# Layer 1's second attention: the last edge type's scores from its weights, and the first softmaxes issued during the last projection

## The chip, the cores and the metric

The kernel runs on one core of a Trainium2 chip. The metric is the device time of one execution in microseconds (us); lower is better. Times given for a kernel are medians over its executions. Beside them stands one profiled execution, in which every instruction has a start and a duration.

The engines are named as in the profile: PE is the matrix engine (TensorE; PEld its weight loads), DVE is VectorE, ACT is ScalarE, POOL is GpSimd, SP is the engine that issues most of the loads. Each engine works through its own list of instructions in order and waits for the others by semaphores.

## The reference

Four graph layers work on 512 nodes with 768 features, over 8704 edges, each followed by a residual sum and a layer norm: a graph attention (layer 0), a relational attention with three edge types (layer 1), a relational convolution (layer 2) and a graph convolution (layer 3). The change is in layer 1, in the second of its two attentions (one head, 768 channels):

```python
def rgat_conv(x, W, q, k, b, src, dst, etype, heads, out_ch, n_nodes):
    xr = jnp.einsum('nd,rdf->rnf', x, W)      # one projection for each edge type r
    oi = xr[etype, dst]
    oj = xr[etype, src]
    alpha = jax.nn.leaky_relu(oi @ q + oj @ k, NEG_SLOPE)
    m = jax.ops.segment_max(alpha, dst, num_segments=n_nodes)
    e = jnp.exp(alpha - m[dst])
    z = jax.ops.segment_sum(e, dst, num_segments=n_nodes)
    a = e / (z[dst] + EPS)
    msg = (a[:, :, None] * oj.reshape(-1, heads, out_ch)).reshape(-1, heads * out_ch)
    return jax.ops.segment_sum(msg, dst, num_segments=n_nodes) + b

h = jax.nn.elu(rgat_conv(x, W1, q1, k1, b1, src, dst, edge_type, 4, 192, n))
out = rgat_conv(h, W2, q2, k2, b2, src, dst, edge_type, 1, 768, n)
```

For each node and each type there are two scores: the query score `xr @ q` of the node as a destination, and the key score `xr @ k` of the node as a source. `xr[r] @ q` is `h @ (W[r] @ q)` as well.

## The kernel before

**Dense form.** The edges have been counted into 512 x 512 matrices, one for each type, whose logarithms (`log3_store`, in device memory) are added to the scores before the exponential. So one softmax step (`soft`) works on a tile of 128 destination nodes by 3 x 512 sources and types: three activations that add a query score as a bias to a row of key scores (L1370), leaky ReLU (L1373), the log and the maximum (L1375), the exponential (L1379). `turn` transposes the 128 x 1536 tile in twelve 128 x 128 steps on PE (L1395) and copies it out of PSUM (L1399). The sum over sources is twelve matmuls against the projected nodes `xr` for each half of the channels (L1522 in the second attention, L1449 in the first).

**Projections.** `product` computes 512 nodes by 384 columns of one weight matrix in four node blocks. A block is twelve matmuls (L799 and L802: rounded parts and remainders, 6 of each), a scale of the PSUM bank on ACT (L805), and six matmuls of a third form (L810, `rest`). The `rest` of one block is issued behind the first twelve matmuls of the next. Behind each block `product` runs a job, if one is given in `between`, and then `split_piece()`, which cuts the next piece of a third of a half weight matrix into its three forms: one activation on ACT (L756) and two steps on DVE (L757, L758), 768 columns each. The raw pieces come over SP's queue into three buffers, the forms live in two sets. A weight matrix is two such units, j = 0 and 1; a PSUM tile is one of eight banks.

**The second attention.** Six products, for types r = 0, 1, 2 and halves j = 0, 1. Each block is copied out of PSUM into `xr[r]`, whose rows are two halves of 384 with columns of ones beside them, by `evacuate`, which alternates between ACT (L85) and DVE (L87). Behind the second half of a type, `dots` computes both scores of a block on DVE: for each score and each half a multiply with an accumulated sum over 128 x 384 (`dot`, L858), and an add of the halves (L1487). After all six products, `on_all` spreads the key scores of each type over all partitions by transposes of broadcast columns (L866), a copy makes them a row (`kk2`), and `run` goes through the softmax steps:

```python
soft_done, turned = {0: soft_of(0)}, {}
for s in range(-1, steps):
    if 0 < s + 2 < steps:
        soft_done[s + 2] = soft_of(s + 2)
    elif s == -1 and steps > 1:
        soft_done[1] = soft_of(1)
    if s + 1 < steps:
        turned[s + 1] = turn(soft_done.pop(s + 1), f"{soft_of.__name__}{s + 1}")
    if s >= 0:
        sum_of(s, turned.pop(s))
```

The log of a step (786 KB) is loaded by SP into a single buffer. `qk2`, the vectors q and k on all partitions, lies in the tile `kk` of the first attention, reused under the same tag; the scratch row of the dots lies under the tag `elu` of the same pool, in a single buffer.

**What sets the order.** The code is issued in program order with few exceptions; a framework places the instructions on their engines, moves some past others by its own estimates, and sets the semaphores. An engine executes the list that comes out of this strictly in order.

Of the kernel before, what the change touches and what calls it, by code (L numbers as in the profile page):

```python
# [34 lines left out]
def gnn_stack_kernel(ctx: ExitStack, tc: tile.TileContext, a: dict, out: bass.AP):  # L35
# [673 lines left out]
    def split_layers():  # L709
# [111 lines left out]
        def columns_of(j):  # L821
            return slice(j * HD, (j + 1) * HD)
# [40 lines left out]
        def on_all(dst, cols, name):  # L863

            for b in range(NB):
                nc.tensor.transpose(  # L866
                    dst[:, b * P : (b + 1) * P], cols[b].to_broadcast([P, P]), ident
                )


        with (
            tc.tile_pool(name="g", bufs=1) as g,
# [148 lines left out]
            class Head:  # L1021
# [8 lines left out]
                def project(self, jobs=(), halves=(0, 1), late=None):  # L1030

                    if late is None and 0 in halves:
                        self.h = [row_tile(f"{self.name}_h{b}") for b in range(NB)]
                    for j in halves:

                        def keep(b, po, j=j):
                            def fill():
                                nc.scalar.copy(self.h[b][:, columns_of(j)], po[:, :HD])

                            if late is not None:  # L1040
                                late.append(fill)
# [12 lines left out]
                    close_group()  # L1054
# [226 lines left out]
        with (  # L1281
# [57 lines left out]
                    f, *args = waiting.pop(0)  # L1339
                    f(*args)  # L1340

            def project(left, r, j, name, also=None):
                def keep(b, po):
                    evacuate(xr[r][:, b, row_slice(j * HD, (j + 1) * HD)], po[:, :HD])
                    if also and j:
                        also(r, b)

                product(left, keep, f"{name}_p{r}_{j}", [next_job] * NB)

            for r in range(R3):  # L1350
                for j in range(2):
# [50 lines left out]
            def source(k, cs):  # L1402
                return xr[k // NB][:, k % NB, cs]

            def run(steps, soft_of, sum_of):


                soft_done, turned = {0: soft_of(0)}, {}
                for s in range(-1, steps):
                    if 0 < s + 2 < steps:  # L1410
                        soft_done[s + 2] = soft_of(s + 2)
                    elif s == -1 and steps > 1:
                        soft_done[1] = soft_of(1)
                    if s + 1 < steps:
                        turned[s + 1] = turn(soft_done.pop(s + 1), f"{soft_of.__name__}{s + 1}")
                    if s >= 0:
                        sum_of(s, turned.pop(s))

            def brow_of(v, name):
                return row_on_all(rp, v, name, "brow")  # L1420
# [15 lines left out]
            def sum1(s, wT):  # L1436
# [29 lines left out]
            run(NB * H1, soft1, sum1)  # L1466
            finish1(NB - 1)

            qk2 = rp.tile([P, H1, R3, N], F32, tag="kk", name="r2_qk").rearrange(
                "p h r n -> p (h r n)"  # L1470
            )
            qk2 = [qk2[:, i * D : (i + 1) * D] for i in range(2)]
            for t, v in zip(qk2, (a["L1_gnn_q2"], a["L1_gnn_k2"])):
                nc.gpsimd.dma_start(t, bass.AP(tensor=v.tensor, offset=v.offset, ap=[[0, P], [1, D]]))
            cols2 = rp.tile([P, 2, R3, NB], F32, tag="cols2", name="r2_cols")
            parts2 = rp.tile([P, 2, 2, R3, NB], F32, tag="parts2", name="r2_parts")

            def dots(r, b):
                for s in range(2):
                    for j in range(2):  # L1480
                        js = row_slice(j * HD, (j + 1) * HD)
                        junk = rp.tile([P, D], F32, tag="elu", name=f"r2_j{r}_{b}_{s}_{j}")
                        dot(
                            parts2[:, j, s, r, b : b + 1], xr[r][:, b, js],
                            qk2[s][:, columns_of(j)], junk[:, :HD],
                        )
                nc.vector.tensor_add(  # L1487
                    cols2[:, :, r, b], parts2[:, 0, :, r, b], parts2[:, 1, :, r, b]
                )

            for r in range(R3):
                for j in range(2):
                    project(S, r, j, "r2", dots)
            close_group()
            kk2 = rp.tile([P, H1, R3, N], F32, tag="kk", name="r2_kk")
            for r in range(R3):
                pk = bank(f"r2_k{r}")
                on_all(pk, [cols2[:, 1, r, b : b + 1] for b in range(NB)], f"r2_k{r}")
                evacuate(kk2[:, 0, r, :], pk)
            brow = brow_of(a["L1_gnn_b2"], "r2_b")  # L1500

            def soft2(b):
                return soft(
                    load_log(b, "r2"), kk2[:, 0], lambda r: cols2[:, 0, r, b : b + 1], f"r2_{b}"
                )

            def finish2(b):
# [297 lines left out]
```

## Time and profile before

| | |
|---|---|
| time before | 1730.66 us, median of 3 (1727.88 to 1731.09) |
| the profiled execution | 1729.9 us, of which its span, first to last instruction, 1727.1 us |
| busy in the span | PE 1614.3, PEld 1443.7, DVE 1187.5, ACT 767.8, POOL 54.2 us |
| projections of the second attention, 937.0 to 1014.2 us | PE busy 77.16 of 77.2, DVE 60.35, ACT 30.27 us |
| from there to the first sum, 1014.2 to 1039.6 us | PE busy 7.32 of 25.4, DVE 17.95, ACT 12.79 us |
| granted TensorE clock, mean | 0.97 |

The page gives for each engine the time in which it executed an instruction; waits are not busy. A list of instructions in order of time gives start, duration, engine, line, operation and operands, and in brackets how long the engine sat idle before it and which instruction released it. The granted clock is the share of full clock that PE was given in a stretch. Line numbers are those of the kernel before; behind line 866 the changed kernel's are some 40 to 60 higher.

### The profile page before, as it was taken

How to read it: one execution, taken by the hardware profiler on the slowest of the kernel's cores; microseconds unless marked ns; L12 is line 12 of the kernel's file. 1: busy time of each engine (PE TensorE's matmuls, PEld its weight loads, DVE VectorE, ACT ScalarE, POOL GpSimd, SP SyncE). 2: the span in 40 equal slices, each digit the busy share in tenths (PEclk: the TensorE clock that was granted, in tenths of full speed). 3: DMA queues.
4: the chain of work that ended last, by engine and by line, in shares of the span. 5: the costliest groups of instructions: out<-in, count | busy, mean ns of one | idle time of the engine just before them, and what ended most of it. 6: DMA issues, size and time to landing. Idle time of an engine off the chain costs nothing.

```text
span 1727.1 us, 22203 instructions
## 1 busy us (share of the span) xinstructions
PE 1614.3 (93%) x8527; PEld 1443.7 (84%) x8527; DVE 1187.5 (69%) x2212; ACT 767.8 (44%) x1321; POOL 54.2 (3%) x71
## 2 busy tenths in 40 slices
PE   5999999999999995999788959999999999999897
PEld 2868879797887964899788956699999999999897
DVE  8977888796868778554784874565666546654764
ACT  5756556554555542243773442233324232423232
POOL 0000000000000002000001000000000002000001
PEclk9999999999999997999799989999999999999999
DMA  3323223131321232222011321232233224332321
GB/s 120 101 71 101 89 89 123 54 103 53 101 64 65 83 91 64 84 74 65 19 38 65 102 82 64 114 119 89 92 104 110 89 80 141 104 95 80 109 63 57
DMA packets 78850, 147.21 MB, mean 85 GB/s; under 512 B 5656, under 2 KB 65936, under 8 KB 76944
## 3 DMA queue, kind: packets, MB, share of 16 engines
q1 hardware_dynamic: 74416, 123.60, 23.2%
q0 software_dynamic: 3600, 20.47, 3.4%
q8 instruction: 69, 1.13, 0.3%
q10 hardware_dynamic: 720, 1.64, 0.3%
q14 instruction: 45, 0.37, 0.1%
HBM read 128.91 MB, written 16.78 MB: 84 GB/s over the span
## 4 chain that ended last, share of the span: by engine, by line
PE 82%; DVE 9%; ACT 4%; DMA 2%; issue 1%; ACTq 0%; DVEq 0%
PE g_o L1061 10%; PE c_p L810 6%; PE c_p L802 6%; PE c_p L799 6%; PE c_a L1565 4%; PE c_a L1569 4%; PE g_s L799 4%; PE g_s L802 4%; PE r_o L1522 4%; PE g_s L810 3%; PE r_p L799 3%; PE r_p L802 3%; PE r_p L810 3%; PE g_p L799 3%; PE g_p L802 3%; PE g_p L810 2%
## 5 line engine op out<-in xcount | busy, mean ns | idle before, releaser
L757 DVE SCALAR_TENSOR_TENSOR w<-w,raw 128x768 fp32r<-128x768 f32 x234 | 222.1, 954 | 116.1 <-ACT w L756 115.0
L756 ACT ACTIVATE w<-raw 128x768 fp32r<-128x768 f32 x234 | 194.8, 839 | 126.2 <-PE c_p L799 34.3
L758 DVE TENSOR_TENSOR w<-w,w 128x768 fp32r<-128x768 f32 x234 | 219.1, 951 | 1.8 <-PE g_p L810 1.0
L802 PE MATMUL c_p<-w,s 128*128 128x384 f32 x576 | 192.5, 334 | 0.0
L799 PE MATMUL c_p<-w,s 128*128 128x384 f32 x576 | 192.5, 334 | 0.0
L1061 PE MATMUL g_o<-wT,g_h 128*128 128x512 f32 x384 | 166.8, 594 | 5.9 <-ACT wT L1017 5.9
L1061 PEld LDWEIGHTS g_o<-wT,g_h 128*128 128x128 f32 x384 | 72.3, 190 | 95.5 <-issue 85.9
L1553 DVE TENSOR_TENSOR c_h_lo<-c_p,c_h_hi 128x384 fp32r<-128x384 f32 x96 | 53.2, 554 | 129.9 <-ACT c_h_hi L1552 129.9
L799 PE MATMUL g_p<-w,s 128*128 128x384 f32 x384 | 134.7, 351 | 0.0
L799 PE MATMUL g_s<-w,y 128*128 128x384 f32 x384 | 131.4, 343 | 0.0
L805 ACT ACTIVATE c_p<-c_p 128x384 f32<-128x384 f32 x96 | 45.6, 475 | 192.9 <-PE c_p L802 192.5
L1565 PE MATMUL c_a<-c_h_hi,c_cT 128*128 128x384 f32 (+1 forms) x384 | 130.5, 340 | 0.0
L802 PE MATMUL g_s<-w,y 128*128 128x384 f32 x384 | 130.0, 339 | 0.0
L802 PE MATMUL g_p<-w,s 128*128 128x384 f32 x384 | 129.7, 338 | 0.1
L1569 PE MATMUL c_a<-c_h_lo,c_cT 128*128 128x384 f32 x384 | 129.8, 338 | 0.0
L810 PE MATMUL c_p<-w,s 128*128 128x384 f32 x576 | 117.9, 339 | 0.0
L799 PEld LDWEIGHTS c_p<-w,s 128*128 128x128 f32 x576 | 108.2, 188 | 0.0
L802 PEld LDWEIGHTS c_p<-w,s 128*128 128x128 f32 x576 | 108.1, 188 | 0.0
L810 PEld LDWEIGHTS c_p<-w,s 128*128 128x128 f32 x576 | 100.0, 188 | 5.3 <-ACT c_p L805 5.3
L799 PE MATMUL r_p<-w,s 128*128 128x384 f32 x288 | 100.0, 347 | 0.0
L802 PE MATMUL r_p<-w,s 128*128 128x384 f32 x288 | 98.5, 342 | 0.0
L810 PE MATMUL g_p<-w,s 128*128 128x384 f32 x384 | 79.4, 340 | 1.5 <-ACT g_p L805 1.4
(259 smaller groups left out, 3278.5 us busy)
## 6 DMA issues: line engine op xcount, KB each, us to landing
raw<-in_L_gnn_W_dram SPq DMA_DIRECT2D x216, 384.0 KB
c_cT<-cT_store POOLq DMA_DIRECT2D x8, 1024.0 KB, 5.7
raw<-in_L_gnn_root_dram SPq DMA_DIRECT2D x18, 384.0 KB
r_log<-log_store SPq DMA_DIRECT2D x8, 768.0 KB
cT_store<-c_cT SPq DMA_DIRECT2D x4, 1024.0 KB
g_s<-in_L_gnn_a_src_dram POOLq DMA_DIRECT2D x8, 384.0 KB, 4.5
g_d<-in_L_gnn_a_dst_dram POOLq DMA_DIRECT2D x8, 384.0 KB, 4.4
log_store<-log SPq DMA_DIRECT2D x12, 256.0 KB
```

The source lines that it names most:

```text
L756: nc.scalar.mul(hm, w, ROUND / SPLIT)
L757: nc.vector.scalar_tensor_tensor(lo, hm, -SPLIT, w, op0=ALU.mult, op1=ALU.add)
L758: nc.vector.tensor_sub(df, hm, lo)
L799: nc.tensor.matmul(po[:, :HD], left[0][:, k, bs], hm[:, k, :], start=(k == 0), stop=False)
L802: nc.tensor.matmul(po[:, :HD], left[1][:, k, bs], lo[:, k, :], start=False, stop=(k == KC - 1))
L805: nc.scalar.mul(po[:, :HD], po[:, :HD], SPLIT + 1.0)
L810: nc.tensor.matmul(po[:, :HD], left[2][:, k, bs], df[:, k, :], start=False, stop=(k == KC - 1), skip_group_check=True,)
L1061: nc.tensor.matmul(po, self.h[k][:, c * P : (c + 1) * P], wT[:, k, :], start=(k == 0), stop=(k == NB - 1),)
L1522: nc.tensor.matmul(po[:, :n], wT[:, k, :], source(k, at), start=(k == 0), stop=(k == NK - 1),)
L1553: nc.vector.tensor_sub(lo, po[:, :HD], hi)
L1565: nc.tensor.matmul(po[:, : HD + ones], cT[:, k, bs], h[0][:, k, : HD + ones], start=(k == 0), stop=False,)
L1569: nc.tensor.matmul(po[:, :HD], cT[:, k, bs], h[1][:, k, :], start=False, stop=(k == NB - 1))
```

## The change

The second attention takes the query and key scores of type 2 no longer from its projected nodes but from its weights. The whole of `W2[2]` (2.36 MB) is loaded a second time, on ACT's queue, into the rest of the tile `kk`, at the end of the first attention. Twelve dots (`last_dots`: six blocks of 128 rows, two scores each) give `W2[2] @ q` and `W2[2] @ k`; `EarlyScores.split` cuts these 128 x 12 numbers into three forms, and `EarlyScores.columns` multiplies them with the forms `S` of all 512 nodes: twelve matmuls with a 2-column stationary tile and 512 moving columns, a scale, six more, a copy, four small transposes. The `dots` of types 0 and 1 work on 768 columns at once, without the adds; those of type 2 are gone. All blocks of the six products are copied out of PSUM by ACT.

The jobs between the blocks issue the rest of it: weight dots during (r, j) = (0, 1) and (1, 0), the score product behind block 2 of (1, 0), the key rows of type 2 behind the first block of (1, 1) and those of types 0 and 1 during (2, 0), softmax steps 0 and 1 during (2, 0), the transposes of step 0 behind block 2 of (2, 1). `run` becomes the class `Steps`, which skips what has been issued. The first attention uses `Steps` too, with nothing issued early.

```diff
+        class EarlyScores:
+            def __init__(self, pool, name):
+                self.name = name
+                self.v = pool.tile([P, 2, KC, 2], F32, tag="early", name=f"{name}_v")
+                self.forms = [
+                    pool.tile([P, KC, 2], F32R, tag=f"early{f}", name=f"{name}_v{f}")
+                    for f in range(3)
+                ]
+
+            def split(self, v):
+                hm, lo, df = self.forms
+                nc.scalar.mul(hm, v, ROUND / SPLIT)
+                nc.vector.scalar_tensor_tensor(lo, hm, -SPLIT, v, op0=ALU.mult, op1=ALU.add)
+                nc.vector.tensor_sub(df, hm, lo)
+
+            def columns(self, left, rows):
+                po = bank(f"{self.name}_r")
+                for k in range(KC):
+                    for f in range(2):
+                        nc.tensor.matmul(
+                            po[:2, :], self.forms[f][:, k, :], left[f][:, k, :],
+                            start=(k + f == 0), stop=(k == KC - 1 and f == 1),
+                        )
+                nc.scalar.mul(po[:2, :], po[:2, :], SPLIT + 1.0)
+                for k in range(KC):
+                    nc.tensor.matmul(
+                        po[:2, :], self.forms[2][:, k, :], left[2][:, k, :],
+                        start=False, stop=(k == KC - 1), skip_group_check=True,
+                    )
+                nc.scalar.copy(rows, po[:2, :])
+                pt = bank(f"{self.name}_c")
+                for b in range(NB):
+                    nc.tensor.transpose(
+                        pt[:, 2 * b : 2 * b + 2], rows[:, b * P : (b + 1) * P], ident[:2, :2]
+                    )
+                return pt[:, : 2 * NB].rearrange("p (b s) -> p s b", s=2)
...
-            def project(left, r, j, name, also=None):
+            def project(left, r, j, name, also=None, jobs=None, copy=evacuate):
                 def keep(b, po):
-                    evacuate(xr[r][:, b, row_slice(j * HD, (j + 1) * HD)], po[:, :HD])
+                    copy(xr[r][:, b, row_slice(j * HD, (j + 1) * HD)], po[:, :HD])
...
-                product(left, keep, f"{name}_p{r}_{j}", [next_job] * NB)
+                product(left, keep, f"{name}_p{r}_{j}", jobs or [next_job] * NB)
...
+            class Steps:
...
+                def run(self):
+                    for s in range(-1, self.steps):
+                        for t in range(s + 3):
+                            self.soft(t)
+                        self.turn(s + 1)
+                        if s >= 0:
+                            self.sum_of(s, self.turned[s])
...
+            both = rp.tile([P, H1 * R3 * N], F32, tag="kk", name="r2_qk")
+            qk2 = [both[:, i * D : (i + 1) * D] for i in range(2)]
+            last_w = both[:, 2 * D :].rearrange("p (c f) -> p c f", f=D)
+            kk2 = both[:, 2 * D : 2 * D + R3 * N].rearrange("p (r n) -> p r n", n=N)
...
+            nc.scalar.dma_start(
+                last_w, a["L1_gnn_W2"][R3 - 1].rearrange("(c p) f -> p c f", p=P)
+            )
...
             def dots(r, b):
                 for s in range(2):
-                    for j in range(2):
-                        js = row_slice(j * HD, (j + 1) * HD)
-                        junk = rp.tile([P, D], F32, tag="elu", name=f"r2_j{r}_{b}_{s}_{j}")
+                    dot(
+                        cols2[:, s, r, b : b + 1], halves(xr[r][:, b, 1 : D + 3], HD + 1),
+                        halves(qk2[s], HD), junk(f"r2_j{r}_{b}_{s}"),
+                    )
+
+            def last_dots(*blocks):
+                for c in blocks:
+                    for s in range(2):
                         dot(
...
+                            early.v[:, 0, c, s : s + 1], halves(last_w[:, c, :], HD),
+                            halves(qk2[s], HD), junk(f"r2_w{c}_{s}"),
+                        )
+
+            def last_scores():
+                early.split(early.v[:, 0])
+                rows = rp.tile([P, D], F32, tag="elu", name="r2_rows")[:2, :N]
+                nc.vector.tensor_copy(cols2[:, :, R3 - 1, :], early.columns(S, rows))
+
+            def keys2(r):
                 pk = bank(f"r2_k{r}")
                 on_all(pk, [cols2[:, 1, r, b : b + 1] for b in range(NB)], f"r2_k{r}")
-                evacuate(kk2[:, 0, r, :], pk)
...
+                nc.scalar.copy(kk2[:, r, :], pk)
...
-            run(NB, soft2, sum2)
+            steps2 = Steps(NB, soft2, sum2)
+            later = {
+                (0, 1): [lambda c=c: last_dots(c) for c in range(4)],
+                (1, 0): [lambda: last_dots(4), lambda: last_dots(5), last_scores],
+                (1, 1): [lambda: keys2(2)],
+                (2, 0): [
+                    lambda: keys2(0), lambda: keys2(1), lambda: steps2.soft(0), lambda: steps2.soft(1)
+                ],
+                (2, 1): [lambda: None, lambda: None, lambda: steps2.turn(0)],
+            }
+            for r in range(R3):
+                for j in range(2):
+                    project(
+                        S, r, j, "r2", dots if r < R3 - 1 else None, later.get((r, j)),
+                        nc.scalar.copy,
+                    )
+            close_group()
+            brow = brow_of(a["L1_gnn_b2"], "r2_b")
+            steps2.run()
             finish2(NB - 1)
```

More of the change, by code (lines that the diff above doesn't have):

```diff
@@ L1403, in source, with __init__, soft, turn @@
                 return xr[k // NB][:, k % NB, cs]
[L1405 to L1417, printed above, removed]
+            class Steps:
+                def __init__(self, steps, soft_of, sum_of):
+                    self.steps, self.soft_of, self.sum_of = steps, soft_of, sum_of
+                    self.soft_done, self.turned = {}, {}
+                def soft(self, s):
+                    if s < self.steps and s not in self.soft_done:
+                        self.soft_done[s] = self.soft_of(s)
+                def turn(self, s):
+                    if s < self.steps and s not in self.turned:
+                        self.turned[s] = turn(self.soft_done[s], f"{self.soft_of.__name__}{s}")
+                def run(self):
[5 more added lines that the diff above has]
+                            self.sum_of(s, self.turned[s])
             def brow_of(v, name):
@@ L1464, in sum1 @@
                     split_piece()
-            run(NB * H1, soft1, sum1)
+            Steps(NB * H1, soft1, sum1).run()
             finish1(NB - 1)
[L1469 to L1472, printed above, removed]
+            both = rp.tile([P, H1 * R3 * N], F32, tag="kk", name="r2_qk")
+            qk2 = [both[:, i * D : (i + 1) * D] for i in range(2)]
+            last_w = both[:, 2 * D :].rearrange("p (c f) -> p c f", f=D)
@@ L1473, in split_layers @@
+            kk2 = both[:, 2 * D : 2 * D + R3 * N].rearrange("p (r n) -> p r n", n=N)
             for t, v in zip(qk2, (a["L1_gnn_q2"], a["L1_gnn_k2"])):
                 nc.gpsimd.dma_start(t, bass.AP(tensor=v.tensor, offset=v.offset, ap=[[0, P], [1, D]]))
+            nc.scalar.dma_start(
+                last_w, a["L1_gnn_W2"][R3 - 1].rearrange("(c p) f -> p c f", p=P)
+            )
             cols2 = rp.tile([P, 2, R3, NB], F32, tag="cols2", name="r2_cols")
-            parts2 = rp.tile([P, 2, 2, R3, NB], F32, tag="parts2", name="r2_parts")
+            early = EarlyScores(rp, "r2")
@@ L1478, in dots, with halves, junk @@
+            def halves(row, c):
+                return row.rearrange("p (j c) -> p j c", c=c)[:, :, :HD]
+            def junk(name):
+                return halves(rp.tile([P, D], F32, tag="elu", name=name), HD)
             def dots(r, b):
                 for s in range(2):
-                    for j in range(2):
-                        js = row_slice(j * HD, (j + 1) * HD)
-                        junk = rp.tile([P, D], F32, tag="elu", name=f"r2_j{r}_{b}_{s}_{j}")
-                        dot(
-                            parts2[:, j, s, r, b : b + 1], xr[r][:, b, js],
-                            qk2[s][:, columns_of(j)], junk[:, :HD],
-                        )
@@ L1487, in dots @@
[L1487 to L1496, printed above, removed]
+                    dot(
+                        cols2[:, s, r, b : b + 1], halves(xr[r][:, b, 1 : D + 3], HD + 1),
+                        halves(qk2[s], HD), junk(f"r2_j{r}_{b}_{s}"),
+                    )
@@ L1497, in split_layers @@
+            def keys2(r):
                 pk = bank(f"r2_k{r}")
                 on_all(pk, [cols2[:, 1, r, b : b + 1] for b in range(NB)], f"r2_k{r}")
-                evacuate(kk2[:, 0, r, :], pk)
-            brow = brow_of(a["L1_gnn_b2"], "r2_b")
+                nc.scalar.copy(kk2[:, r, :], pk)
             def soft2(b):
                 return soft(
-                    load_log(b, "r2"), kk2[:, 0], lambda r: cols2[:, 0, r, b : b + 1], f"r2_{b}"
+                    load_log(b, "r2"), kk2, lambda r: cols2[:, 0, r, b : b + 1], f"r2_{b}"
```

## The prediction

> **What bounds the kernel now.** I read the page first: busy shares, then the 40 slices.
>
> ```profile
> span 1727.1 us, 22203 instructions
> ...
> PE 1614.3 (93%) x8527; PEld 1443.7 (84%) x8527; DVE 1187.5 (69%) x2212; ACT 767.8 (44%) x1321; POOL 54.2 (3%) x71
> ...
> PE   5999999999999995999788959999999999999897
> ```
>
> TensorE is the bound nearly everywhere, so an edit pays only where PE is idle. Slice 23 (993 to 1036 us) shows 5: it is the end of the third projection of layer 1's second attention. Next, busy time by stretch: the whole projection, the hole behind it, the first sum.
>
> ```profile
> core 0: us, PE busy (x) PEld busy (x) DVE busy (x) ACT busy (x) POOL busy (x), PEclk, DMA share, GB/s
> 937.00:1014.20 77.20, 77.16 (x438) 76.81 (x437) 60.35 (x139) 30.27 (x56) 3.86 (x2) 0.98 0.27 83
> 1014.20:1039.60 25.40, 7.32 (x36) 6.20 (x35) 17.95 (x31) 12.79 (x18) 0.00 (x0) 0.61 0.34 109
> 1039.60:1055.40 15.80, 15.80 (x51) 9.26 (x50) 7.40 (x10) 5.12 (x6) 0.00 (x0) 0.98 0.16 50
> ```
>
> PE is full for 77.2 us, then works 7.3 of 25.4. In PE's order of time (start, duration, instruction, idle before and its releaser):
>
> ```profile
> 1018.48 0.32 PE L866 MATMUL r_k<-ident,r_cols 128*128 128x128 f32 x1 [3.15 <-DVE r_cols L1487]
> 1022.45 0.47 PE L866 MATMUL r_k<-ident,r_cols 128*128 128x128 f32 x1 [3.65 <-DVE r_cols L1487]
> 1030.63 2.82 PE L1395 MATMUL soft_wt<-ident,r_z 128*128 128x128 f32 x12 [7.71 <-ACT r_z L1379]
> 1037.02 2.82 PE L1395 MATMUL soft_wt<-ident,r_z 128*128 128x128 f32 x12 [3.57 <-ACT r_z L1379]
> ```
>
> The hole is a chain: last dots on VectorE, key rows, first softmax, its transposes, second softmax, its transposes, first sum at 1039.64. The change must fill these 25.4 us. VectorE meanwhile has free time early, while it waits for ACT's next weight pieces:
>
> ```profile
> 940.48 0.56 DVE L780 SCALAR_TENSOR_TENSOR s<-s,s 128x384 fp32r<-128x384 f32 x1
> 944.77 0.56 DVE L858 CUSTOM_DVE_ANT_0 r_j<-xr,r_qk 128x384 f32<-128x384 f32 x1 [3.73 <-ACT xr L85]
> 950.16 0.96 DVE L757 SCALAR_TENSOR_TENSOR w<-w,raw 128x768 fp32r<-128x768 f32 x1 [2.23 <-ACT w L756]
> ```
>
> **The change, part by part.** Times below are on the clock of the profiled execution. I followed each engine's order of instructions in the changed build and laid the measured durations along it. (r, j) is half j of the projection of type r, in four node blocks of 18 matmuls, 3.12 us each.
>
> *Start.* Late in the first attention, VectorE's last ELU step of node block 2 (L1463) is issued behind a reciprocal, a transposed copy (L1399) and a row update (L1455). PE waits for it at 917.21. Spacings 0.08 + 0.59 + 0.34 put it 1.0 us later. All later times move by +1.0.
>
> *Load.* One more DMA (2.36 MB) on ACT's queue at about 914, between two ELU activations; DMA issues on that queue took 0.27 to 0.56 us at the start of the program, and VectorE's next work there is busy until 916.1 anyway: zero. The engines were idle from 922 to 934 here, and one-microsecond stretches elsewhere reach 412 GB/s. At even 150 GB/s it lands by 930 to 935; the first user, VectorE at 937.4, needs it then. If late, the split of node block 3 (L779) queues behind it, and PE needs that only at 948.
>
> *Dots.* What a 768-wide dot costs:
>
> ```profile
> L858 DVE CUSTOM_DVE_ANT_0 r_j<-xr,r_qk x48: 548/554/560, 944.8 to 1021.6; 128x384 f32<-128x384 f32 x48
> L858 DVE CUSTOM_DVE_ANT_0 g_j<-g_h,g_s x32: 950/952/960, 68.7 to 587.1; 128x768 bf16<-128x768 f32 x32
> ```
>
> 48 half dots, 12 adds (0.16 us) and 12 copies (L87, 0.56 us) leave VectorE; 28 dots of 768 come (16 on nodes, 12 on weights). In all it saves about 9 us, but the place decides. Two weight dots run at 937.4. The next weight dots stand behind the split of the weights of (1, 0), which waits for ACT until 951, so VectorE's free time above stays empty. From ACT's copy of the first second-half block (958.2) there are 24 operations in a row: 8 node dots, 10 weight dots, 6 split steps (0.95 us each). A dot behind a dot waits for the shared junk row: 0.99 us apart (0.60 for half dots now, i.e. 0.04 over the duration), otherwise 0.87. So 11 x 0.99 + 12 x 0.875 + 1.0 = 22.4 us: end at 980.7, rounded part on ACT (one small activation, 0.3): 981.0.
>
> *Score product.* PE's order puts it after block 2 of (1, 0), whose last matmul ends at 974.35 (973.3 + 1.04, with the +1.0). PE then waits for the weights' scores: 981.0 - 974.35 = **6.65 us of stall**. Queued behind it on PE are block 3 and all later projections; behind it on ACT (the small activation waits for VectorE too) the split of the weights of (2, 0). Then a serial block: 12 matmuls 128x512, ACT's scale, 6 matmuls, ACT's copy, 4 tiny transposes. Six 384-wide ones take 1.04, so a 512-wide one 0.231 us at full clock. But what does the clock do after a stall?
>
> ```profile
> 936.00:937.00 1.00, 0.41 (x4) 1.00 0.42 141
> 938.00:939.00 1.00, 1.00 (x5) 0.50 0.54 120
> 941.00:942.00 1.00, 1.00 (x7) 0.95 0.00 0
> ```
>
> (PE alone: length, PE busy, granted clock, DMA.) After 3.8 us of idle the clock fell to 0.50 for about 3.2 us, and matmuls stood 0.32 instead of 0.17 apart. [...] I take 4.9, as the row agrees. Rest: two ACT steps with their hand-overs 2 x 0.65 (0.47 us for 384 columns, 0.58 for 512), 6 x 0.23 = 1.4, transposes and hand-over 0.6. **Score product 8.2 us.** No row shows 2-column stationary tiles; bounds 5.5 (full clock) to 10 (half clock throughout).
>
> *Last projections.* 12 key transposes x 0.12 = 1.4 us and 24 softmax transposes at full clock 2 x 1.3 = 2.7 us now lie among them. The key row of type 1 needs the last node dot of type 1: VectorE reaches it at 1012.2, PE at 1012.3: zero, up to 2. ACT carries all 24 evacuations (12 x 0.47 us more) and softmax 0 and 1 in (2, 0) and (2, 1): 8 scales and 8 copies of 0.41, 6 split pieces 0.78, 9 bias activations 0.65, 2 exponentials 1.57, 4 copies 0.55: 22 of 27 us. Its exponential of softmax 1 waits for the second log tile; the single buffer is free when VectorE is done with the first (1019), SP's issue stands behind three root-weight pieces already freed, landing 4.7 us later as now (1028.9 to 1033.6). Behind that exponential on ACT stands the scale of block 2 of (2, 1), which PE wants only at 1030.6. But the biases of softmax 2 (3 x 0.65) and a split piece stand ahead of the scale of block 3: PE waits **1.2 us** (bounds 0 and 4).
>
> *Sum.* First projection matmul to first sum is now 1039.64 - 937.19 = 102.45. Changed: 77.0 (projections) + 1.0 + 6.65 + 8.2 + 1.4 + 2.7 + 1.2 = 98.15. Difference **-4.3 us**. After 1039.64 PE is full either way: nothing more. The profiled execution took 1729.9 (span 1727.1 and 2.8 around it): 1725.6. It lies 0.76 below the median of the runs shown, 1730.66, from which I forecast 1726.4. A measurement of this kernel can tell about 0.2%, 3.5 us, from no change.
>
> **The rivals.**
>
> *A, the scores come nearly free (chance 0.20).* Stall 3 us, score product 5.5 at full clock, no slip on ACT: 6.65 - 3 + 2.7 + 1.2 = 7.6 more: 1718.8; half of this 1722.5. For: the whole hole is 25 us. Against: VectorE's 24 operations leave no slack.
>
> *B, ACT becomes the bound of the last projection (0.14).* Each scale and copy waits behind bias and exponential activations up to 2 us long. Four such waits of about 1 us: 1730.4, no change. For: about 80% busy there, in order. Against: most scales have a block (2.1 us) of room.
>
> *C, slower (0.14).* The row of dots before the score product ends later. Place: VectorE from 958 to 981, 18 dots; each us there is a us of stall on PE. If a dot over two halves of a padded row with an f32 junk row costs 1.55 instead of 0.95, the stall grows by 10.8: 1737.2. The gain is gone at 0.24 us more per dot, slower by over 0.2% from 0.43. For: L780 took 1.72 instead of 0.56 us beside GpSimd's add. Against: those adds end by 943, and the 384-wide rows show f32 and bf16 junk alike (0.554).
>
> That the change does not do what it says: the first softmaxes do stand ahead of the last projection's end in the order; only a wait could undo it, which B and C hold.
>
> **How the numbers follow.** Main case 0.52: 1726.4, its own range 1723 to 1729.5 from the bounds above. Faster by over 0.2% (below 1727.1): two thirds of the main case and A, 0.34 + 0.20 = 0.54. Within: the rest of it and most of B, 0.30. Slower: C and a little of B, 0.16. The range reaches to the middle of A and half-way into C: 1718 to 1734.
>
> **What would show it.** Right: PE idle before the score product of 5 to 8 us, released by ACT; granted clock 0.50 in it; first sum near 1035 on this clock; no hole over 2 us between the last projection and the sum. Wrong: dots of clearly over 0.99 us apart, several waits of scales on ACT, or a score product that finds its weights ready.

## The result, and the profile after

The changed kernel takes **1726.06 us**, median of 20 runs (1720.58 to 1731.76); the kernel before, beside it, 1731.01 (20 runs, 1727.53 to 1733.85). The ratio is 0.9974, 95% interval 0.9965 to 0.9983: a small gain, 5 us. The profiled execution took 1724.68 us, 5.2 less than that of before, but its span is only 4.2 shorter. The other 1.0 us lies outside the span, that is, outside the time from the first to the last instruction: in all 20 runs of the changed kernel the time exceeds the span by 1.8 to 1.9 us, in 52 runs of the kernel before by 2.7 to 3.1. All the kernels below have 1.7 to 1.9, the one with the side parts alone too; where this microsecond comes from is not shown. First the page: span, busy times, slices.

```profile
span 1722.9 us, 22204 instructions
...
PE 1617.1 (94%) x8549; PEld 1441.6 (84%) x8549; DVE 1182.5 (69%) x2150; ACT 774.9 (45%) x1337; POOL 55.1 (3%) x71
...
PE   5989999999999995999788899999999999999897
```

The total of PE's busy time rose by 2.8 us while the span fell by 4.2. The 5 in slice 23 has become a 9, and the 9 before it an 8. The stretch from the first projection matmul to the first sum, by windows (the columns stand in the first line):

```profile
core 0: us, PE busy (x) PEld busy (x) DVE busy (x) ACT busy (x) POOL busy (x), PEclk, DMA share, GB/s
936.50:970.40 33.90, 33.90 (x189) 33.90 (x188) 22.79 (x39) 14.22 (x27) 4.38 (x2) 0.95 0.23 71
...
972.70:979.70 7.00, 0.00 (x1) 0.00 (x1) 6.40 (x15) 0.69 (x2) 0.00 (x0) 0.86 0.09 35
979.70:988.30 8.60, 7.24 (x23) 2.30 (x24) 0.39 (x3) 1.12 (x2) 0.00 (x0) 0.71 0.00 0
988.30:1034.50 46.20, 46.16 (x274) 44.94 (x275) 35.61 (x47) 33.01 (x57) 0.00 (x0) 1.00 0.37 115
```

The hole behind the projections is gone: from 988.3 to 1034.5 PE is busy 46.16 of 46.20 us. In its place PE does nothing at all for 7.00 us, at 972.7, while DVE is at work for 6.40 of them. The waits of PE from 936 to 1036 us (who waited, for whom, total us, how often, longest):

```profile
PE r_r L893 <- ACT r_v L883: 7.0, 1, 7.0
PE x1b_t L770 <- DVE r_y L1514: 3.8, 1, 3.8
PE r_r L899 <- ACT r_r L897: 0.7, 1, 0.7
PE r_c L906 <- ACT r_rows L903: 0.7, 1, 0.7
```

The second line is the wait in front of the projections, which was there before. The other three belong to the score product. In PE's order of time:

```profile
979.70 5.18 PE L893 MATMUL r_r<-s,r_v 128*2 128x512 f32 x12 [7.02 <-ACT r_v L883]
985.57 1.55 PE L899 MATMUL r_r<-s,r_v 128*2 128x512 f32 x6 [0.70 <-ACT r_r L897]
987.79 0.41 PE L906 MATMUL r_c<-ident,r_rows 2*128 2x2 f32 x4 [0.67 <-ACT r_rows L903]
...
1032.23 1.36 PE L1436 MATMUL soft_wt<-ident,r_z 128*128 128x128 f32 x11
1033.43 15.67 PE L1584 MATMUL r_o<-xr,soft_wT 128*128 128x385 f32 x48
```

The first projection matmul started at 936.53, the first sum at 1033.43: **96.90 us** where it was 102.45, so 5.55 less. It balances like this. Idle time of PE inside the stretch fell from 18.1 us (25.40 - 7.32) to 8.4 (7.02 + 0.70 + 0.67): -9.7. The score product keeps PE busy for 7.1 us that were not there: it lasts from 979.70 to the next projection matmul at 988.13, 8.43, less its two inner waits. And the two groups of softmax transposes now run at full clock (granted 1.00 where it was 0.50), 1.4 us each in place of 2.82: -2.9. Together -5.5. In front of the stretch 0.8 us is lost to the late ELU step (below): from the softmax transposes ahead of node block 2's transposes to the first projection matmul it is 24.39 us in place of 23.60. For the two together that makes -4.8 us. Outside of them, where nothing was changed, the two traces differ by -1.5 us ahead and +2.0 us behind.

### The profile page after: what moved, and what is told of

Same layout as the page of the kernel before. It is cut to its first block, busy times and chain, and to the rows that moved or that the text cites. A ratio compares the mean times of both kernels' runs of the same rounds, so it can differ in the third digit from the quotient of the medians.

```text
span 1722.9 us, 22204 instructions
## 1 busy us (share of the span) xinstructions
PE 1617.1 (94%) x8549; PEld 1441.6 (84%) x8549; DVE 1182.5 (69%) x2150; ACT 774.9 (45%) x1337; POOL 55.1 (3%) x71
## 4 chain that ended last, share of the span: by engine, by line
PE 82%; DVE 10%; ACT 4%; DMA 2%; issue 1%; ACTq 0%; DVEq 0%
PE g_o L1102 10%; PE c_p L810 6%; PE c_p L802 6%; PE c_p L799 6%; PE c_a L1645 4%; PE c_a L1649 4%; PE g_s L799 4%; PE g_s L802 4%; PE r_o L1584 4%; PE g_s L810 4%; PE g_p L799 3%; PE r_p L799 3%; PE g_p L802 3%; PE r_p L802 3%; PE r_p L810 3%; PE g_p L810 2%
```

## The experiments

Each kernel ran beside the kernel before on the same chip; a time stands beside that chip's own time of before.

### All weight dots early

The theory: the 7 us stall is VectorE's row of operations, which starts only when ACT has copied out the first second-half block, and ten of its dots are weight dots that nothing tied to that place. Put them where VectorE had free time.

```diff
-                (0, 1): [lambda c=c: last_dots(c) for c in range(4)],
-                (1, 0): [lambda: last_dots(4), lambda: last_dots(5), last_scores],
+                (0, 0): [lambda: last_dots(0, 1), lambda: last_dots(2, 3), lambda: last_dots(4, 5)],
+                (1, 0): [lambda: None, lambda: None, last_scores],
```

> The changed kernel, with the twelve dots on the weights issued during (0, 0) instead of during (0, 1) and (1, 0), so that VectorE does them in its idle time between 940 and 950 us. Theory (VectorE's dots end 7 us after PE wants their result, and PE then runs the score product at half clock, in one serial piece): the stall of 7.0 us goes, the first twelve matmuls of the score product take 2.8 instead of 5.2 us, and other matmuls come to stand between its steps, 1 us: 10 to 11 us less than the changed kernel, about 1715.5. Rival (another wait of the last projections, on ACT, takes its place): PE waits later, in (1, 1) to (2, 1), and the time stays within 3 us of the changed kernel's 1726.

Measured: 1712.5 us (1709.3 to 1715.62, 4 runs; before 1730.66), ratio 0.9895 (0.9877 to 0.9914). PE's list of this kernel at the same place:

```profile
969.31 2.94 PE L893 MATMUL r_r<-s,r_v 128*2 128x512 f32 x12
972.95 1.55 PE L899 MATMUL r_r<-s,r_v 128*2 128x512 f32 x6
975.17 0.41 PE L906 MATMUL r_c<-ident,r_rows 2*128 2x2 f32 x4 [0.31 <-ACT r_rows L903]
...
1020.82 15.66 PE L1584 MATMUL r_o<-xr,soft_wT 128*128 128x385 f32 x48
```

No bracket behind the first line: the stall is gone, and nothing took its place. The twelve matmuls take 2.94 us in place of 5.18, and the wait of 0.70 after them is filled with projection matmuls. First projection matmul (935.94) to first sum: 84.88 us, 12.0 less than in the changed kernel. The stall (7.02), the clock (2.24) and the inner waits (1.06) make 10.3 of this. Nearly all of the rest is luck: the first 24 projection matmuls took 4.25 us in this execution, at full clock, and 5.82 in the changed kernel's, at half clock for more than half of it. Another trace of the same kernel, further down, has 86.43 us, 10.5 less, which is what was expected.

One of the moved dots (939.70) took 2.60 us in place of 0.96, beside an add on GpSimd from 939.41 to 941.49. It cost nothing here, because VectorE had the room.

### The score product half a projection later

The same question from the other side: leave the dots, ask for the product later.

```diff
-                (1, 0): [lambda: last_dots(4), lambda: last_dots(5), last_scores],
-                (1, 1): [lambda: keys2(2)],
+                (1, 0): [lambda: last_dots(4), lambda: last_dots(5)],
+                (1, 1): [lambda: None, last_scores, lambda: None, lambda: keys2(2)],
```

> The changed kernel, with the score product issued behind block 1 of (1, 1) instead of block 2 of (1, 0), and the key rows of type 2 two blocks later; the dots stay where they are. Theory: PE gets there at about 981 us, when the dots are just done, so the stall shrinks from 7.0 to at most 1 us and the clock is full; the score product stays serial, about 6 us: 8.5 to 9.5 us less than the changed kernel, about 1717. Rival (the late key row of type 2 delays the first softmax, and PE waits at its transposes): no more than 3 us less.

Measured: 1720.76 (1714.55 to 1724.54, 4 runs; before 1730.66), ratio 0.9947 (0.993 to 0.9963). That is 5.3 us less than the changed kernel: between the theory (8.5 to 9.5) and the rival (at most 3), whose reason is not there, since PE never waited for the late key row. PE's list says what the theory missed, and VectorE's says why:

```profile
979.87 0.40 PE L893 MATMUL r_r<-s,r_v 128*2 128x512 f32 x1 [0.66 <-ACT r_v L883]
981.45 4.27 PE L893 MATMUL r_r<-s,r_v 128*2 128x512 f32 x11 [1.19 <-DVE r_v L884]
```

```profile
978.61 0.95 DVE L858 CUSTOM_DVE_ANT_0 r_w<-r_qk 128x768 f32<-128x768 f32 x1
...
979.49 0.95 DVE L757 SCALAR_TENSOR_TENSOR w<-w,raw 128x768 fp32r<-128x768 f32 x1
980.36 0.95 DVE L858 CUSTOM_DVE_ANT_0 r_j<-xr,r_qk 128x768 f32<-128x768 f32 x1
981.23 0.08 DVE L858 DVE_READ_ACCUMULATOR2_ANT r_cols<- 128x1 f32 x1
981.23 0.17 DVE L884 SCALAR_TENSOR_TENSOR r_v<-r_v,r_v 128x12 fp32r<-128x12 f32 x1
```

The last weight dot here ends at 979.6, as late as in the changed kernel: node dots and split steps of the next weights were issued between the weight dots. And the small step L884 (0.17 us), which makes the second form of the weights' scores, stands behind a split step and a node dot of 0.95 each. PE needed it for its second matmul. The eleven matmuls after that wait ran at half clock for most of the time (4.27 us, 0.39 each). So the stall fell by 5.2 us, to 0.66 + 1.19, but the clock that the theory had counted as full did not come: twelve matmuls in 4.67 us in place of 5.18. The stretch took 91.27 us, 5.63 less than in the changed kernel. (It is the stretch that can be compared here: this execution, 1714.55 us, was the fastest of four that lie 10 us apart.)

### The scores alone

How much does the early scoring cost, and how much do the early softmaxes bring? Here the scores of type 2 come from the weights as in the change, but key rows, softmax steps and transposes stay behind the projections.

```diff
-                (1, 1): [lambda: keys2(2)],
-                (2, 0): [
-                    lambda: keys2(0), lambda: keys2(1), lambda: steps2.soft(0), lambda: steps2.soft(1)
-                ],
-                (2, 1): [lambda: None, lambda: None, lambda: steps2.turn(0)],
...
+            for r in range(R3):
+                keys2(r)
```

> The changed kernel without its early issue: scores of type 2 from the weights as there, but all key rows and all softmax steps behind the last projection. Theory (two parts of opposite sign): the stall and the score product stay, and the hole behind the projections comes back, less the time in which the last dots held it: 17 us from the end of the projections to the first sum. First sum 13 to 14 us later than in the changed kernel: about 1739.5, slower than before by 8 to 9. Rival (the scores themselves bring the gain, since the chain of the last dots is gone): no slower than before, 1726 to 1731.

Measured: 1742.48 (1738.93 to 1746.6, 4 runs; before 1730.66), ratio 1.007 (1.005 to 1.009); slower than before, and 3 us above what was expected. PE's waits from the first projection to the first sum:

```profile
PE soft_wt L1436 <- ACT r_z L1420: 11.8, 2, 8.3
PE r_r L893 <- ACT r_v L883: 7.0, 1, 7.0
```

The chain of softmaxes is still there in full (11.3 us in the kernel before), the stall has come on top. Only the waits for the key rows are gone, 6.8 us before. The stretch took 111.3 us, 14.4 more than in the changed kernel (expected: 13 to 14); most of the 3 us are outside it. So the early softmaxes alone are worth 16.4 us (1742.48 to 1726.06; 14.4 by the two traces' stretches), and the price paid to make them possible was some 12 (1730.66 to 1742.48).

### The side parts alone

The kernel before with dots of 768 columns and all copies out of PSUM on ACT, and nothing else of the change.

```diff
-            def project(left, r, j, name, also=None):
+            def project(left, r, j, name, also=None, copy=evacuate):
...
-                    for j in range(2):
-                        js = row_slice(j * HD, (j + 1) * HD)
...
+                    dot(
+                        cols2[:, s, r, b : b + 1], halves(xr[r][:, b, 1 : D + 3], HD + 1),
+                        halves(qk2[s], HD), halves(junk, HD),
+                    )
...
-                    project(S, r, j, "r2", dots)
+                    project(S, r, j, "r2", dots, nc.scalar.copy)
```

> The kernel before, with two side parts of the change alone: dots of 768 columns without the adds, and all blocks of the six products copied out of PSUM by ACT. Theory: VectorE's row at the end of the last projection gets shorter by some 3 us of work, of which about 2 are seen, since six split steps still stand among the dots: 1 to 3 us less than before, about 1729. Rival (the side parts bring what the change brings): 4 to 5 us less than before, about 1726.

Measured: 1728.66 (22 runs; before 1730.66), ratio 0.999 (0.9982 to 0.9998): about 2 us, of which 1.0 is the time outside the span named above. The waits of PE in the stretch:

```profile
PE soft_wt L1395 <- ACT r_z L1379: 11.3, 2, 7.8
PE r_k L866 <- DVE r_cols L858: 5.2, 2, 3.2
```

The chain of softmaxes is untouched; the last dots end a little earlier, so the key rows wait 5.2 us in place of 6.8. (The stretch, 99.39 us, is 3.1 shorter than before. The other half of this is again the luck of the clock: the first 24 projection matmuls ran at full clock in this trace and took 4.27 us.)

### Six more weight dots

Rival C's mechanism by hand: lengthen VectorE's row on purpose. The repeats write the same values again.

```diff
-                (1, 0): [lambda: last_dots(4), lambda: last_dots(5), last_scores],
+                (1, 0): [lambda: last_dots(4, 4), lambda: last_dots(5, 5, 5), last_scores],
```

> The changed kernel with six more weight dots of 768 in the row before the score product (blocks 4 and 5 dotted two and three times over; the repeats write the same values). Theory (VectorE's row of dots sets the stall one for one): each repeat is 0.99 us, so the row ends 6.0 us later, TensorE's idle time before the score product grows from 7.0 to 13.0 us, and the time from 1726.1 to about 1732. Rival (some of the row is slack, the stall is set by the arrival of the rounded part on ScalarE or by TensorE's own order): the stall grows by less than 4 us, time below 1730. Rival (a longer stall also costs clock or a late split of the next weights): more than 8 us, above 1734.

Measured: 1731.91 (1727.92 to 1737.75, 12 runs; before 1730.78), ratio 1.001 (0.9999 to 1.0021). The wait, in its trace:

```profile
PE r_r L893 <- ACT r_v L883: 13.0, 1, 13.0
```

Six dots, 6.0 us of stall, 6.1 us of stretch (103.01 for 96.90), 5.9 us of time over the changed kernel's 1726.06: one for one, and the whole gain of the change is gone. The row had no slack.

### Something for PE to do in the stall

Are the 5.18 us of the first twelve matmuls the clock, or the two-column stationary tiles? Matmuls that nobody reads fill the stall and leave the stall itself as it is.

```diff
             def last_scores():
+                fill = bank("r2_fill")
+                for i in range(36):
+                    nc.tensor.matmul(
+                        fill[:, :HD], S[0][:, i % KC, :P], S[1][:, i % KC, :HD], start=True, stop=True
+                    )
                 early.split(early.v[:, 0])
```

> The changed kernel with 36 matmuls of 128x384 that nobody uses put on TensorE into the idle time before the score product (36 x 0.174 = 6.3 us of 7.0). Theory (the first 12 matmuls of the score product take 5.2 us because the clock fell during the stall): they now take 2.8 to 2.9 us at clock 1.0, and the time falls by 2.3 us to about 1723.7. Rival (the 5.2 us belong to matmuls with two-column stationary tiles): they still take about 5 us, time 1726. Rival (the filler itself ends late): if it runs over the stall by more than 2 us, no gain or a loss.

Measured: 1722.94 (1721.73 to 1725.3, 4 runs; before 1730.78), ratio 0.9954 (0.9937 to 0.9971). PE's list:

```profile
975.22 6.40 PE L1557 MATMUL r_fill<-s,s 128*128 128x384 f32 x36
981.46 1.21 PE L810 MATMUL r_p<-w,s 128*128 128x384 f32 x6
983.45 2.95 PE L893 MATMUL r_r<-s,r_v 128*2 128x512 f32 x12 [0.79 <-ACT r_v L883]
```

The stall is the same: 6.24 us of filler up to 981.46 and the 0.79 us left over make 7.03. The twelve matmuls take 2.95 us, and from their start to the first sum it is 51.50 us in place of 53.73: 2.23 less. The 5.18 us were the clock. (The median fell by 3.1 us, within the spread of four runs.)

### The second read on SP's queue

```diff
-            nc.scalar.dma_start(
+            nc.sync.dma_start(
                 last_w, a["L1_gnn_W2"][R3 - 1].rearrange("(c p) f -> p c f", p=P)
             )
```

> The changed kernel with the second read of the last weights issued on SyncE's queue in place of ScalarE's. In the order of VectorE's instructions the last ELU step of node block 2 then stands where it stood before the change. Theory (the change costs 1.0 us in front of the projections because that ELU step is issued later): TensorE's wait for it falls from 3.1 to about 2.1 us, and the time by 1.0 us to about 1725. Rival (the load on ScalarE's queue itself delays ScalarE): the same gain but with a ScalarE gap gone near 911 us. Rival (run to run spread): the wait stays at 3 us, time 1726.

Measured: 1723.93 (1722.89 to 1727.47, 5 runs; before 1730.78), ratio 0.9959 (0.9945 to 0.9973). The wait in front of the transposes of node block 2, first in the changed kernel, then here:

```profile
916.73 1.51 PE L770 MATMUL x1b_t<-ident,r_y 128*128 128x128 f32 x6 [3.12 <-DVE r_y L1514]
```

```profile
918.94 0.94 PE L770 MATMUL x1b_t<-ident,r_y 128*128 128x128 f32 x6 [2.13 <-DVE r_den L1427]
```

VectorE's list around that ELU step (L1514), again the changed kernel first:

```profile
914.65 0.08 DVE L1416 DVE_READ_ACCUMULATOR2_ANT r_nmax<- 128x1 f32 x1
...
915.64 0.95 DVE L1514 SCALAR_TENSOR_TENSOR r_y<-r_e,r_y 128x768 f32<-128x768 f32 x1
```

```profile
917.84 0.08 DVE L1416 DVE_READ_ACCUMULATOR2_ANT r_nmax<- 128x1 f32 x1
917.84 0.95 DVE L1514 SCALAR_TENSOR_TENSOR r_y<-r_e,r_y 128x768 f32<-128x768 f32 x1
```

The step is back in its old place and the wait back at 2.13. The order of VectorE's list was the cause, and the queue on which the DMA was issued decided that order. The issue did not delay ACT itself: from the exponential to the first ELU activation behind it ACT needs 1.48 us with the issue between them and without it.

Not all of the microsecond is seen in the time. In this trace matmuls ran at half clock behind the shorter wait as well, for longer: from its end to the next softmax transposes it took 6.28 us in place of 6.09, and behind the next wait (3.80) the first projection matmul came after 1.16 us in place of 0.60. From the softmax transposes to the first projection matmul it took 24.17 us, 0.2 less than the changed kernel's 24.39; with the early dots and SP's queue (below) it took 23.61, as in the kernel before (23.60). The time of one variant alone is within its spread; the wait is what shows it.

### What can be added to the early dots

Three variants on the early dots: with the score product in three parts behind blocks 1, 2 and 3 of (1, 0), with the read on SP's queue, and with both. The early dots ran once more beside two of them.

```diff
-                early.split(early.v[:, 0])
-                rows = rp.tile([P, D], F32, tag="elu", name="r2_rows")[:2, :N]
-                nc.vector.tensor_copy(cols2[:, :, R3 - 1, :], early.columns(S, rows))
+                early.split(early.v[:, 0])
+                early.columns(S)
+
+            def last_rest():
+                rows2.append(rp.tile([P, N], F32, tag="early_rows", name="r2_rows")[:2, :])
+                early.rest(S, rows2[0])
+
+            def last_turn():
+                nc.vector.tensor_copy(cols2[:, :, R3 - 1, :], early.turned(rows2[0]))
...
+                (1, 0): [lambda: None, last_scores, last_rest, last_turn],
```

Both together:

> All weight dots in the first half projection of type 0, the score product issued in three parts behind blocks 1, 2 and 3 of half projection (1, 0) so that ScalarE's two steps between its parts lie under projection blocks, and the second read of the weights on SyncE's queue. Theory: against the variant with early dots alone (1712.5) the last 0.3 us of wait before the tiny transposes goes and 1.0 us in front of the projections: about 1711.3. Rival (with the stall gone something else in the stretch is late: ScalarE's weight pieces, or the clock): 1712.5 or above.

Measured: 1714.19 (1713.74 to 1715.22, 4 runs; before 1730.78), ratio 0.9908 (0.9891 to 0.9924). The time lies where the rival put it, but its reason, a new wait, is not there: PE's only one in the stretch was 0.2 us for a scale on ACT. The next three ran on one chip (before 1728.55) to see whether the split or the queue costs something.

> The variant with all weight dots early, once more, on the same chip as the two that follow, to set its spread. From its first median, 1712.5: 1711 to 1714.5 if the spread there was only run to run. Of the two theories for the early-and-split variant (1714.2): if the split or the other queue costs something, this one stays about 1.5 us below it; if the half-clock stretches after TensorE's waits (of unequal length from run to run) made the difference, the medians of the three lie within 1.5 us of one another, in the order of what each removes.

Measured: 1715.37 (1714.33 to 1717.79, 5 runs), ratio 0.9924 (0.991 to 0.9937).

> Early dots, and the second read of the last weights on SyncE's queue, the score product in one piece. Theory (the late ELU step is worth 1.0 us, as the wait of 2.1 instead of 3.1 us showed): 1.0 us below the early dots alone on the same chip. Rival (the half clock that follows either wait takes the microsecond back): no difference, within 0.5 us.

Measured: 1712.24 (1710.73 to 1712.74, 4 runs), ratio 0.9902 (0.9887 to 0.9917).

> Early dots, the score product in three parts behind blocks 1, 2 and 3 of half projection (1, 0), the read on ScalarE's queue as in the changed kernel. Theory (the split removes a wait of 0.3 us and meets another of 0.2 us): equal to the early dots alone within 0.5 us. Rival (the split costs: a tail of the score product now meets ScalarE's softmax work): 1.5 us above.

Measured: 1713.1 (1711.41 to 1717.22, 5 runs), ratio 0.9915 (0.9901 to 0.9929); no wait of PE in the stretch at all.

None of the three came out as expected. The early dots lie above their range (1711 to 1714.5), SP's queue gave 3.1 us on the same chip in place of 1.0, and the split 2.3 in place of nothing. The traces say where the differences are. The middle column is the part that these edits touch, from the softmax transposes ahead of node block 2's transposes to the first sum (us of the span; the last column is the time of the execution):

| | ahead of it | this part | behind it | time |
|---|---|---|---|---|
| early dots, first run | 913.0 | 107.8 | 688.1 | 1710.64 |
| early dots, again | 915.7 | 110.9 | 688.2 | 1716.57 |
| SP's queue | 914.3 | 110.0 | 686.6 | 1712.74 |
| in three parts | 912.8 | 110.2 | 686.5 | 1711.41 |
| both | 915.6 | 109.8 | 686.6 | 1713.74 |

Against the early dots run again, the part itself is 0.9 us shorter with SP's queue, 0.7 with the split and 1.1 with both: within 0.4 us of the waits that were to go; so nothing here says that the split or the queue costs anything. The larger part of the differences between these executions lies ahead of this part and behind it, where none of these kernels was edited. The one kernel that ran twice gave 1712.5 and 1715.37, a wider step than between any two of the variants. The 3.1 us by which its first trace is faster in this part are the luck of the clock: half of them in front of the projections, half in the first matmuls, as told for the first run.

The 1.6 us behind this part are the clock too. PE has a wait of 2.88 us there, before the transposes of the next layer. Both times the early dots ran, half clock followed it (matmuls of the next layer 0.32 us apart); in the other three full clock did (0.17 to 0.18 us apart). Early dots first, then with SP's queue:

```profile
1090.46 1.45 PE L770 MATMUL x_t<-ident,r_y 128*128 128x128 f32 x6 [2.88 <-DVE r_y L834]
```

```profile
1093.99 0.85 PE L770 MATMUL x_t<-ident,r_y 128*128 128x128 f32 x6 [2.89 <-DVE r_y L834]
```

All four kernels beat the changed kernel and the one before, the latter by 0.8 to 1.0%. Which of them is best is not settled by these runs.

## Why the prediction was right, step by step

- **The sum.** Forecast 1726.4 us, measured 1726.06. For the stretch from the first projection to the first sum the terms made 97.15 (98.15 with the ELU step in front of it); measured 96.90. That the times agree to 0.3 us is luck in part. The gain was forecast at 4.3 us and measured at 4.95, and 1.0 of this is the time outside the span, which the forecast took to stay at 2.8 us. Single runs of the changed kernel lie up to 11 us apart. The firm part is the trace: -4.8 us from the softmax transposes ahead of the ELU step's wait to the first sum, with -4.3 forecast.
- **Start, +1.0.** The transposes of node block 2 came 4.59 us after the softmax transposes ahead of them began, in place of 3.62: +0.97, and +0.79 at the first projection matmul. The order of VectorE's list was the reason, as the read on SP's queue showed by taking it back.
- **Load, zero.** Nobody waited for it. Its issue (0.39 us, at 911.31) fell beside an exponential of ACT and put nothing off there, and DVE's first weight dot (935.81) ran without a wait.
- **Dots.** The row is the step on which everything hung:

```profile
949.49 0.96 DVE L757 SCALAR_TENSOR_TENSOR w<-w,raw 128x768 fp32r<-128x768 f32 x1 [9.14 <-ACT w L756]
...
956.69 0.96 DVE L858 CUSTOM_DVE_ANT_0 r_j<-xr,r_qk 128x768 f32<-128x768 f32 x1 [1.05 <-ACT xr L1385]
...
978.43 0.96 DVE L858 CUSTOM_DVE_ANT_0 r_w<-r_qk 128x768 f32<-128x768 f32 x1
```

  VectorE's free time stays empty, as forecast (9.14 us), and then it works from 956.69 to 979.39, 22.7 us for 22.4. A dot over two halves with an f32 scratch row costs 0.96 us, as the row of the unsplit dots had said; so rival C's dearer dot did not come in this row. Its rate did: the six extra dots cost 6.0 us.
- **Stall, 6.65.** Measured 7.02: 0.3 of the row and 0.1 of the hand-over.
- **Score product, 8.2.** Measured 8.43, and the point that was argued most held: half clock. PE alone, in windows of a microsecond (length, PE busy, granted clock, DMA):

```profile
977.00:978.00 1.00, 0.00 (x0) 0.90 0.00 0
978.00:979.00 1.00, 0.00 (x0) 0.50 0.00 0
...
983.00:984.00 1.00, 1.00 (x4) 0.50 0.00 0
984.00:985.00 1.00, 0.88 (x3) 0.69 0.00 0
985.00:986.00 1.00, 0.43 (x2) 1.00 0.00 0
```

  The clock fell during the stall and rose again only at the end of the twelve matmuls: 5.18 us (taken: 4.9). The 4.9 was an estimate of the author's. The row shown for it, half clock for 3.2 us, would give about 4.2: 7.5 matmuls at 0.427 us (0.32 x 512/384) and 4.5 at 0.231; all twelve at 0.231 make 2.8. In the three other traces with a stall of 7 or 13 us they took 5.11 to 5.28, and 2.94 and 2.95 where PE had work ahead of them. The choice between 4.9 and 2.8 was worth 2.2 us as measured, almost half of the gain.
- **Transposes, 1.4 + 2.7 at full clock.** Right: 1.36 for 11 softmax transposes, and no key row waited.
- **Slip on ACT, 1.2.** This term was wrong: PE never waited for a scale in the last projection. It was the price given to rival B, and with it B is out. The misses on the other side (0.4 in the stall, 0.2 in the product, and 0.35 over the 77.0 that are left for the projections) make up for most of it, by luck.
- **Rival A** (the scores nearly free) is what the early dots made of it: stall 0, product at full clock. It needed the dots in another place, not faster dots. Its 1718.8 was too high, since it left 3 us of stall and the product in one piece.

All the signs named for being right came: 7.02 us of idle PE, released by ACT, a granted clock of 0.50 behind it, and no hole between the last projection and the sum. What the forecast saw but did not draw out: it named VectorE's free time (now 9.14 us) beside the row that was too long. To move the ten dots from the one to the other was worth more than the change itself.

## What to carry to other kernels

Work that is moved early to break a chain is itself a chain: ask which of its inputs comes last, and on which engine's list that input's work stands behind something else. Here the change paid 12 us to move a softmax worth 16, and most of the price was ten dots that stood behind an unrelated wait and could be issued one product earlier.

When a stall on the matrix engine is priced, price also the work right behind it at half clock. Here half clock stood behind stalls of 7 and 13 us in every trace (twelve matmuls in 5.11 to 5.28 us in place of 2.94), and behind waits of 3.12 us in seven of eight (six transposes in 1.51 us in place of 0.85). Filler matmuls show how much of it is the clock: here they brought the twelve to 2.95.

## What the runs showed of the hardware

What the half clock costs behind the same waits differed from trace to trace by 3.5 us, as much as a measurement of this kernel can tell. The wait of 3.12 us in front of node block 2's transposes was followed by full clock in one trace and by half clock for over 6 us in another. First the early dots, then the kernel with the filler (length, PE busy, granted clock, DMA):

```profile
918.00:919.00 1.00, 1.00 (x10) 1.00 0.96 381
```

```profile
917.00:918.00 1.00, 0.06 (x1) 0.52 1.00 412
918.00:919.00 1.00, 1.00 (x5) 0.50 1.00 399
...
923.00:924.00 1.00, 1.00 (x5) 0.57 1.02 393
```

Between the start of the softmax transposes ahead of this wait and the first projection matmul lay 22.90 us in the first case and 26.37 in the second, with the same instructions and waits: 2.9 us of the difference stand behind the wait of 3.12 us and 0.6 behind a second one of 3.79. The changed kernel had 24.39, and so had the five others with that wait, within 0.15. The profiled early dots were the lucky case: they lie near the low end of that kernel's runs.

How long the clock stayed down can be estimated from the rows, if a window with a value between 0.50 and 1.00 is taken as a mix of the two. A window of 1 us at 0.52 was then at half clock for all but 0.04 us, one at 0.57 for all but 0.14, so with the filler the half clock lasted from 917.04 to 923.86, 6.8 us. The rows of the changed kernel's stall (0.90 and 0.69) give 977.80 to 984.62, 6.8 us as well. Behind its wait of 3.12 us it was half as long:

```profile
916.00:917.00 1.00, 0.27 (x2) 0.68 1.04 421
917.00:918.00 1.00, 1.00 (x6) 0.50 0.99 390
918.00:919.00 1.00, 1.00 (x5) 0.50 1.05 433
919.00:920.00 1.00, 1.00 (x5) 0.61 1.03 424
```

These rows give 916.36 to 919.78, 3.4 us. So the same wait was followed by 0, 3.4 or 6.8 us of half clock in these three traces; what decides it is not shown. Such places in the program may be a source of the spread of 6 to 11 us between runs of the kernels that ran most often, larger than several of the differences sought here. The softmax transposes ahead of node block 2 began between 909.28 us (late product) and 915.73 us (early dots, again), where both kernels had done the same work. An estimate from the rows of the first 900 us, busy time times the missing share of the clock, has 11.2 us lost to the lowered clock in the first and 18.8 in the second (mean granted clock of the two whole executions: 0.979 and 0.974). Over all the traces the two go together only in part, and no run tried it by itself.

Half clock came behind less idle time than that, too. In the kernel with the late product two waits of 0.66 and 1.19 us had 0.4 us of work between them (979.2 to 981.45):

```profile
981.00:982.00 1.00, 0.55 (x3) 0.92 0.51 97
...
985.00:986.00 1.00, 0.72 (x3) 0.87 0.00 0
```

By these rows the clock was at 0.50 from 981.84 to 985.26, 3.4 us, behind 1.85 us of idle time in all. With the filler, waits of 0.79, 0.70 and 0.67 us, 1.5 to 3 us of work between them, left the whole product at full clock: 2.95, 1.55 and 0.41 us for its three groups of matmuls, as in the early dots (2.94, 1.55, 0.41).
